# An adaptive-norm state-space block on one Trainium2 core: the small matmuls of a quad of head pairs in three atomic sections

## The chip, the core and the metric

The kernel runs on one core of a Trainium2 chip: TensorE (PE) with its weight loads (PEld), VectorE (DVE), ScalarE (ACT), GpSimd (POOL), and SyncE (SP), whose queue here issues the DMAs. TensorE writes its results to PSUM[...]. The metric is the device time of one execution in microseconds (us); the median of the runs counts.

## The reference

For 4 batches of 512 tokens with 256 channels: a normalisation with a shift and a scale from a small modulation network, a state-space mixer, a gated residual, a second normalisation, a feed-forward layer with a Hadamard transform, a second gated residual. The mixer is where the change lies:

```python
proj = u @ W_in.T
xBC, z, A_log = jnp.split(proj, [CONV_DIM, CONV_DIM + D_INNER], axis=-1)
...
x = x.reshape(b, l, NH, HEADDIM)
Bm = Bm.reshape(b, l, NH, D_STATE)
Cm = Cm.reshape(b, l, NH, D_STATE)
a = -jax.nn.softplus(A_log).transpose(0, 2, 1)
Lm = jnp.exp(segsum(a))
M = jnp.einsum('blhn,bshn,bhls->bhls', Cm, Bm, Lm)
y = jnp.einsum('bhls,bshp->blhp', M, x)
y = y + D[None, None, :, None] * x
```

There are 32 heads of 8 channels with a state of 64. Before this, xBC passes a causal convolution of four taps along the tokens.

## The kernel before

Everything is float32. The sum over earlier tokens is cut into 8 chunks of 64 tokens. Within a chunk the product of C and B, times the decays, is applied to x (**intra**). Across chunks, each chunk gives a state (**states**), the states are carried on by a scan (**turn_states**), and the products of C with the carried state are added (**inter**).

Work comes in *pairs* of heads, k = 0 to 63. Four pairs make a *quad*, m = 0 to 15; two quads make a *unit*, n = 0 to 7, which is half of the heads of one batch. For a pair:

- `project` (lines 447 to 455) computes B (half 0, PSUM tile pbc) and C (half 1, pcc), each by six full matmuls 512 wide (line 266), and `conv` (400 to 407) applies the convolution: two ACT operations from PSUM, two DVE operations, one POOL operation. The results are bc (3 buffers) and cc (8 buffers).
- `turn_b` (475 to 481) transposes B into bts (tag bt, 6 buffers).
- `prep_l` (440 to 445) makes the decays lts (tag l, 6 buffers): one matmul, one exponential on ACT.
- `attend` (457 to 473), once for two pairs, multiplies C and B chunk by chunk in two m banks (pG): 4 matmuls per chunk, 32 in all, each on a 64 by 64 piece of the array. A class `Chain` keeps them in order among themselves; other matmuls may come between. DVE then multiplies pG into lts (line 473).

For a quad: `states` (540 to 550) runs 16 matmuls on 128 by 32 pieces into one m bank (ps), and ACT copies it to st; `intra` (552 to 565) runs 32 on 128 by 32 pieces into the unit's bank py; `turn_states` (567 to 579) transposes st, scans it on DVE, and POOL writes it to sts; `inter` (581 to 591) runs 28 on 128 by 32 pieces into the unit's bank pi. A float32 matmul shows as two instructions in the trace, so a quad has 32 ps, 64 py and 56 pi, and an `attend` 64 pG.

PSUM: three banks for projections (tag p), three for everything of short life (tag m: pG, ps, the transposes bT, sT, xt and pt, the decays pl, the output products), one each for py and pi.

The order is made in two steps. The code is traced by an agenda: each piece has a due time in units of a pair (table `T`, line 414, and lines 784 to 841), and the pieces are traced in order of due time. Then a scheduler that models the engines' times orders each engine's instructions: among those whose inputs and buffers are there, the earlier traced goes first. So a later piece can slip into an earlier one. Only SP keeps its traced order. Where a tag has no free buffer, the writer waits until all readers of an old one are done.

Due times for quad m: states at 4m + 3.97, intra at 4m + 4.1, turn_states at 4m + 5.47, inter at 4m + 6.53. For pair k: attend (k odd) at k + 0.12, turn_b at k + 0.13, the projections at k - 1.11 and k - 1. After the mixer, the feed-forward part (from line 706) fills the last 135 us.

Of the kernel before, what the change touches and what calls it, by code (L numbers as in the profile page):

```python
# [16 lines left out]
AF = mybir.ActivationFunctionType  # L17
# [6 lines left out]
Q = 64  # L24
NC = S // Q
# [5 lines left out]
def mamba_ffn(tc, ctx, u, c_t, wmod, win_t, cw, cb, zb, dsk, wo_t, w13_t, w2_t,  # L31
              k_ident, k_reset, k_dl, k_dr, k_had, k_own, out):
    nc = tc.nc
    ve, ac, gp, pe = nc.vector, nc.scalar, nc.gpsimd, nc.tensor
# [14 lines left out]
    def at_time(t, fn, *args):  # L49
        heappush(agenda, (t, next(ids), fn, args))  # L50
# [9 lines left out]
    def work(shape, name, tag, bufs=2, dtype=F32):  # L60
        return wk.tile(shape, dtype, name=name, tag=tag, bufs=bufs)

    def mtile(shape, name):
        return ps_m.tile(shape, F32, name=name, tag="m")
# [97 lines left out]
    xpad = const.tile([128, 2, NC, 4, 32], F32, name="xpad")  # L162
    sts = [const.tile([128, NC - 1, 4, 32], F32, name=f"sts{pp}") for pp in range(2)]
    xwz = const.tile([128, 4, 16, 2, 8], F32, name="xwz")
# [100 lines left out]
        for n, (a, b, k) in enumerate(TERMS):  # L265
            last[pe] = pe.matmul(ps, w[:, a, k, c0 : c0 + 128], ht[k][:, b], start=(n == 0), stop=(n == 5))  # L266

    class Chain:

        def __init__(self):  # L270
            self.before = None

        def matmul(self, *args, **kw):
            with ExitStack() as order:
                if self.before is not None:
                    order.enter_context(tc.issue_after(self.before.ins))
                self.before = pe.matmul(*args, **kw)  # L277

    def normalize(b, which, x):
        mv = work([128, 4, 2], f"mv{which}{b}", "mv")  # L280
        rs = work([128, 4], f"rs{which}{b}", "rs")
        xn = work([128, 4, DM], f"xn{which}{b}", "xn", 1)
        for t in range(4):
            bs = work([128, 6], f"bs{which}{b}{t}", "bs")
            ve.bn_stats(bs, x[:, t])
            ve.bn_aggr(mv[:, t], bs)
        ve.tensor_scalar(rs, mv[:, :, 1], EPS, None, ALU.add)
        last[gp] = gp.tensor_tensor(rs, rs, neghalf, ALU.pow)
        if (b, which) == (0, 0):
            for t in range(4):  # L290
                ve.tensor_scalar(xn[:, t], x[:, t], mv[:, t, 0:1], rs[:, t : t + 1], ALU.subtract, ALU.mult)
            return xn
        nm = work([128, 4], f"nm{which}{b}", "nm")
        ve.scalar_tensor_tensor(nm, mv[:, :, 0], -1.0, rs, ALU.mult, ALU.mult)
        for t in range(4):
            ac.activation(xn[:, t], x[:, t], AF.Identity, bias=nm[:, t : t + 1], scale=rs[:, t : t + 1])  # L296
        return xn
# [102 lines left out]
    def conv(ps, tl, dst):  # L400
# [9 lines left out]
    NP = 64  # L410
# [2 lines left out]

    T = dict(
        attend=0.12, turn_b=0.13, prep_l=-1.31, proj_b=-1.11, proj_c=-1, load_d=-3.13,
        states=-0.03, intra=0.1, turn=1.47, inter=2.53,
        x_proj=1.32, x0=-1.5, x1=2.12, x2=3.46, x3=3.77, gate_z=5.89, fin0=3.54, fin1=3.96, fin2=4.99, fin3=6.63,
        pro0=-11.83, pro1=-7.06, pro2=-4.93, pro3=-4.48, pro4=-3.88, next_ht=-3.77, pro04=0.27,
        quads=1.55, xz1=32.3, wo=19.68, mod=18.99, w2=40.89, wf0=56.74, wf1=62.02, wf2=62.29,
        load_w2=63.01, w2tag=1, w2gp=0, first_h2=59.14, lag=4.89, next_h2=-2.27,  # L420
    )
# [5 lines left out]
    lts, bcs, ccs, bts, exs, des, xcs, xds, dcs, stt, pys, zts = ({} for _ in range(12))  # L427
# [29 lines left out]
    def attend(k):  # L457


        ks = (k - 1, k)  # L460
        pgs = [mtile([128, S], f"pG{n}") for n in ks]
        chain = Chain()
        for c in range(NC):


            for n, pg in list(zip(ks, pgs))[::-1]:
                for j in range(2):
                    i, o = 64 * j, 64 * (j ^ (n % 2))
                    r, l = slice(i, i + 64), slice(Q * c, Q * c + Q)
                    chain.matmul(pg[o : o + 64, l], bcs[n][r, l], ccs[n][r, l], start=True, stop=True,  # L470
                                 tile_position=(i, o))
        for n, pg in zip(ks, pgs):
            ve.tensor_tensor(lts[n], pg, lts[n], ALU.mult)  # L473

# [62 lines left out]
                                 wdec[b][:, 2 * hf + t, :, 16 * i : 16 * i + 16]  # L537
                                 .unsqueeze(3).to_broadcast([128, 2, 16, 8]), ALU.mult)

    def states(m):  # L540
        pp = m % 2
        pst = mtile([128, 4, 128], f"ps{m}")
        for t in range(4):
            for g in range(4):
                pe.matmul(pst[32 * g : 32 * g + 32, t], xwz[:, t, 4 * g + 2 * pp : 4 * g + 2 * pp + 2].rearrange("p h q x -> p (h q x)"),  # L545
                          bts[4 * m + g][:, t], start=True, stop=True, tile_position=(0, 32 * g))
        for g in range(4):
            bts.pop(4 * m + g)
        stt[m] = work([128, 4, 128], f"st{m}", "st", 1)
        ac.activation(stt[m], pst, AF.Copy)  # L550

    def intra(m):
        n, pp = divmod(m, 2)
        if pp == 0:
            pys[n] = (ps_1.tile([128, S], F32, name=f"py{n}", tag="y"),
                      ps_1.tile([128, S], F32, name=f"pi{n}", tag="yi"))
        py = pys[n][0]
        for c in range(NC):
            for g in range(4):
                l = slice(Q * c, Q * c + Q)  # L560
                pe.matmul(py[32 * g : 32 * g + 32, l], xpad[:, pp, c, g], lts[4 * m + g][:, l],  # L561
                          start=(pp == 0 and c == 0), stop=(pp == 1), skip_group_check=True,
                          tile_position=(0, 32 * g))
        for g in range(4):
            lts.pop(4 * m + g)

    def turn_states(m):
        n, pp = divmod(m, 2)
        st = stt.pop(m)
        pt = mtile([128, 4, 16, NC], f"sT{m}")  # L570
        for t in range(4):
            pe.transpose(pt[:, :, :, 2 * t : 2 * t + 2].rearrange("p g (h x) q -> p (g h) q x", h=2), st[:, t], ident)
        sn = work([128, 4, 16, NC], f"sn{m}", "xd", 2)
        ve.tensor_tensor_scan(sn.rearrange("p g x c -> p (g x c)"),
                              dcs[n][:, 8 * pp : 8 * pp + 8].rearrange("p h x c -> p (h x c)"),
                              pt.rearrange("p g x c -> p (g x c)"), 0.0, ALU.mult, ALU.add)
        o = 16 * pp
        gp.tensor_tensor(sts[pp][:, :, :, o : o + 16].rearrange("p c g x -> p g x c"), sn[:, :, :, : NC - 1],
                         own.unsqueeze(3).to_broadcast([128, 4, 16, NC - 1]), ALU.mult)

    def inter(m):
        n, pp = divmod(m, 2)
        pi = pys[n][1]
        for c in range(1, NC):
            for g in range(4):
                l = slice(Q * c, Q * c + Q)
                pe.matmul(pi[32 * g : 32 * g + 32, l], sts[pp][:, c - 1, g], ccs[4 * m + g][:, l],  # L587
                          start=(pp == 0 and c == 1), stop=(pp == 1), skip_group_check=True,
                          tile_position=(0, 32 * g))
        for g in range(4):  # L590
            ccs.pop(4 * m + g)

    def gate_z(n):
        i, b = units[n]
        pz = ptile(f"pz{n}")
        proj(pz, wxz[i], 128, ht[i, b])
        zt = work([128, S], f"zt{n}", "zt", 1)
        zz = work([128, S], f"zz{n}", "zz", 1)
        ac.activation(zt, pz, AF.Tanh, bias=hzb[:, i : i + 1], scale=0.5)
        ac.activation(zz, pz, AF.Identity, bias=zb_sb[:, i : i + 1])  # L600
        ve.scalar_tensor_tensor(zt, zt, 1.0, zz, ALU.add, ALU.mult)
        zts[n] = zt
# [179 lines left out]
        split_xz(1, fetch_xz(1))  # L782

    for m in range(16):
        at_time(4 * m + 4 + T["states"], states, m)
        at_time(4 * m + 4 + T["intra"], intra, m)
        at_time(4 * m + 4 + T["turn"], turn_states, m)
        at_time(4 * m + 4 + T["inter"], inter, m)
        if m:
            at_time(4 * m + T["load_d"], load_d, m)  # L790
    for k in range(NP):
        if k % 2:
            at_time(k + T["attend"], attend, k)
        at_time(k + T["turn_b"], turn_b, k)
        if k >= AHEAD:
            at_time(k + T["proj_b"], project, k, 0)
            at_time(k + T["proj_c"], project, k, 1)
        if k >= LOOK_P:
            at_time(k + T["prep_l"], prep_l, k)
# [106 lines left out]
```

## Time and profile before

| | us |
|---|---|
| median of 3 runs | 590.82 |
| lowest, highest | 587.2, 591.58 |
| the profiled execution | 587.27 |
| its span, first to last instruction | 585.5 |
| busy over the span: PE, PEld | 547.6, 431.7 |
| busy over the span: DVE, ACT, POOL | 400.5, 392.8, 325.6 |

A busy time is the sum over an engine's instructions; overlapping matmuls are counted once. Lines of groups and timelines name the source line (L277), the engine, the operation, the tile written and the tiles read, and the sizes; for matmuls "64*64" is the piece of the array in use. In the views of waits a line says which instruction stood still, which engine and tile released it, and the total, the number of times and, where there is a third number, the longest time.

### The profile page before, as it was taken

The page shows a single profiled execution, that of the slowest core. Times are in us where ns is not written, and L with a number is a line of the kernel's source. Part 1 is how long each engine was busy: PE and PEld are TensorE (multiplying, and loading weights), DVE is VectorE, ACT ScalarE, POOL GpSimd, SP SyncE. Part 2 cuts the span into 40 slices and gives each one's busy share as a digit, 9 for nine tenths or more (in the row PEclk, how much of TensorE's full clock was granted, in tenths as well). Part 3 has the DMA queues.
Part 4 walks back from the last instruction along what each step waited for, and adds up shares of the span by engine and source line. Part 5 has one row for each costly group of instructions (what it writes and reads, how often), then busy time and mean ns, then how long its engine had stood idle before and what let it go on. Part 6 is the DMA issues. An engine that isn't in the chain of part 4 may idle for free.

```text
span 585.5 us, 16297 instructions
## 1 busy us (share of the span) xinstructions
PE 547.6 (94%) x6868; PEld 431.7 (74%) x6868; DVE 400.5 (68%) x668; ACT 392.8 (67%) x670; POOL 325.6 (56%) x299
## 2 busy tenths in 40 slices
PE   6887999989899999999999899899989999999996
PEld 3555776668677766877777677677767898888886
DVE  4777877877787875889787879787855454333243
ACT  6898778877967887897794887769574243232321
POOL 4773356454734578466565657477666645333341
PEclk9898999999999999999999999999989999999999
DMA  6423111210325344013203142164158046104021
GB/s 195 137 53 151 33 37 74 47 34 1 110 50 84 115 123 142 3 59 103 80 4 113 75 119 97 60 172 147 38 158 284 2 131 209 40 1 152 1 82 36
DMA packets 41792, 51.99 MB, mean 89 GB/s; under 512 B 17942, under 2 KB 29940, under 8 KB 41720
## 3 DMA queue, kind: packets, MB, share of 16 engines
q1 hardware_dynamic: 40248, 50.58, 28.6%
q8 instruction: 54, 0.88, 0.6%
q10 hardware_dynamic: 1472, 0.38, 0.3%
q14 instruction: 18, 0.15, 0.1%
HBM read 33.51 MB, written 17.44 MB: 87 GB/s over the span
## 4 chain that ended last, share of the span: by engine, by line
PE 40%; DVE 5%; ACT 4%; issue 1%; POOL 1%; DMA 1%; POOLq 0%; DVEq 0%
PE f L266 15%; PE pdy L728 4%; PE pcc L266 4%; PE pdyi L728 4%; PE pbc L266 3%; PE po L625 2%; PE pG L277 1%; PE py L561 1%; PE bT L479 1%; ACT xn L296 1%; PE ps L545 1%; PE pi L587 1%; DVE cc L405 1%; PE pt L306 1%; ACT cv L404 1%
## 5 line engine op out<-in xcount | busy, mean ns | idle before, releaser
L407 POOL TENSOR_TENSOR bc<-bc,cv 128x509 f32<-128x509 f32 x64 | 69.6, 1088 | 58.7 <-DVE bc L406 41.4
L266 PE MATMUL f<-h,wf 128*128 128x512 f32 x384 | 97.3, 395 | 0.0
L407 POOL TENSOR_TENSOR cc<-cc,cv 128x509 f32<-128x509 f32 x64 | 69.7, 1089 | 49.2 <-DVE cc L406 33.4
L266 PEld LDWEIGHTS f<-h,wf 128*128 128x128 f32 x384 | 69.0, 189 | 12.3
L721 POOL TENSOR_TENSOR fl<-ft,fh 128x512 fp32r<-128x512 f32 x31 | 40.0, 1292 | 57.6 <-ACT fh L720 52.0
L405 DVE SCALAR_TENSOR_TENSOR cc<-pcc,cw_sb,cc 128x511 f32<-128x511 f32 x64 | 47.6, 743 | 31.0 <-ACT cv L404 30.9
L402 ACT ACTIVATE cc<-pcc,cb_sb,cw_sb 128x512 f32<-128x512 f32 x64 | 50.2, 785 | 20.6 <-PE pcc L266 15.1
L266 PE MATMUL pcc<-ht,wq 128*128 128x512 f32 x192 | 55.5, 421 | 5.8 <-DVE bc L406 5.8
L402 ACT ACTIVATE bc<-pbc,cb_sb,cw_sb 128x512 f32<-128x512 f32 x64 | 50.1, 783 | 15.3 <-PE pG L277 14.0
L720 ACT ACTIVATE fh<-ft 128x512 fp32r<-128x512 f32 x32 | 20.2, 631 | 57.7 <-DVE ft L717 28.7
L716 DVE SCALAR_TENSOR_TENSOR ft<-ft,f 128x512 f32<-128x512 f32 x32 | 21.9, 687 | 52.2 <-ACT ft L715 50.0
L405 DVE SCALAR_TENSOR_TENSOR bc<-pbc,cw_sb,bc 128x511 f32<-128x511 f32 x64 | 47.6, 744 | 12.8 <-ACT cv L404 12.6
L266 PE MATMUL pcc<-hr,wq 128*128 128x512 f32 x192 | 53.3, 410 | 2.9 <-DVE bc L406 2.3
L266 PE MATMUL pbc<-ht,wq 128*128 128x512 f32 x192 | 53.0, 408 | 2.6 <-POOL wq L199 2.6
L266 PE MATMUL pbc<-hr,wq 128*128 128x512 f32 x192 | 52.4, 406 | 1.4 <-DVE cc L406 1.0
L266 PEld LDWEIGHTS pcc<-ht,wq 128*128 128x128 f32 x192 | 35.8, 196 | 18.0 <-DVE bc L406 8.0
L406 DVE SCALAR_TENSOR_TENSOR bc<-pbc,cw_sb,bc 128x510 f32<-128x510 f32 x64 | 47.6, 743 | 1.2
L406 DVE SCALAR_TENSOR_TENSOR cc<-pcc,cw_sb,cc 128x510 f32<-128x510 f32 x64 | 47.6, 744 | 1.1
L473 DVE TENSOR_TENSOR l<-pG,l 128x512 f32<-128x512 f32 x64 | 41.2, 683 | 7.8 <-PE pG L277 7.5
L479 PE MATMUL bT<-ident,bc 128*128 128x128 f32 x256 | 41.2, 283 | 4.3 <-ACT bt L481 2.6
L404 ACT ACTIVATE cv<-pbc,cw_sb 128x512 f32<-128x512 f32 x64 | 44.4, 693 | 1.4 <-POOL bc L407 0.9
L481 ACT ACTIVATE bt<-bT 128x512 f32<-128x512 f32 x64 | 38.8, 607 | 9.4 <-PE bT L479 9.2
(154 smaller groups left out, 1237.0 us busy)
## 6 DMA issues: line engine op xcount, KB each, us to landing
wq<-win_t SPq DMA_DIRECT2D x16, 256.0 KB
htd<-ht SPq DMA_DIRECT2D x8, 512.0 KB
hr<-htd SPq DMA_DIRECT2D x8, 512.0 KB
h2d<-ht SPq DMA_DIRECT2D x8, 512.0 KB
h<-h2d SPq DMA_DIRECT2D x8, 512.0 KB
x<-u SPq DMA_DIRECT2D x7, 512.0 KB
ex<-pd SPq DMA_DIRECT2D x8, 256.0 KB
ygd<-yg SPq DMA_DIRECT2D x4, 512.0 KB
```

What stands on the lines that cost most here:

```text
L266: last[pe] = pe.matmul(ps, w[:, a, k, c0 : c0 + 128], ht[k][:, b], start=(n == 0), stop=(n == 5))
L402: ac.activation(dst, ps, AF.Identity, bias=cb_sb[:, tl : tl + 1], scale=w[:, 3:4])
L404: last[ac] = ac.activation(v, ps, AF.Copy, scale=w[:, 0:1])
L405: ve.scalar_tensor_tensor(dst[:, 1:], ps[:, : S - 1], w[:, 2:3], dst[:, 1:], ALU.mult, ALU.add)
L406: last["conv"] = ve.scalar_tensor_tensor(dst[:, 2:], ps[:, : S - 2], w[:, 1:2], dst[:, 2:], ALU.mult, ALU.add)
L407: last[gp] = gp.tensor_tensor(dst[:, 3:], dst[:, 3:], v[:, : S - 3], ALU.add)
L473: ve.tensor_tensor(lts[n], pg, lts[n], ALU.mult)
L479: pe.transpose(pt[:, t], bc[:, 128 * t : 128 * t + 128], ident)
L481: ac.activation(bts[k], pt, AF.Copy)
L716: ve.scalar_tensor_tensor(t, t, 1.0, p1, ALU.add, ALU.mult)
L721: (ve if (b, f) == (NB - 1, 7) else gp).tensor_tensor(lo, t, hi.bitcast(F32), ALU.subtract)
L728: last[pe] = pe.matmul(pds[t // 2][:, t % 2], hid[a][:, tok], w2h[f][:, w_], start=(f == 0 and t % 2 == 0 and m == 0), stop=(f == 7 and m ...
```

## The change

`states` and `intra` become one function, `states_intra`, whose matmuls are in one atomic section: to the scheduler it is a single unit that nothing can be put between, that starts when all its inputs are there, and that is done when all of it is. `attend` gets such a section around its matmuls in place of `Chain`. In every second `attend` of a quad, from the second quad on, the section begins with `inter` of the quad before; the last quad's `inter` has a section of its own. The due time of states goes, that of intra serves both; inter has a due time of its own only for the last quad. C's buffers are released behind the section (`drop_c`). The matmuls, their number and their data are the same.

```diff
-    class Chain:
...
-        states=-0.03, intra=0.1, turn=1.47, inter=2.53,
+        intra=0.1, turn=1.47, inter=2.53,
...
         pgs = [mtile([128, S], f"pG{n}") for n in ks]
-        chain = Chain()
-        for c in range(NC):
-            for n, pg in list(zip(ks, pgs))[::-1]:
-                for j in range(2):
...
-                    chain.matmul(pg[o : o + 64, l], bcs[n][r, l], ccs[n][r, l], start=True, stop=True,
-                                 tile_position=(i, o))
+        m = (k - 7) // 4 if k % 4 == 3 else -1
+
+        with tc.tile_critical():
+            if m >= 0:
+                inter(m)
+            for c in range(NC):
+                for n, pg in list(zip(ks, pgs))[::-1]:
+                    for j in range(2):
...
+                        pe.matmul(pg[o : o + 64, l], bcs[n][r, l], ccs[n][r, l], start=True, stop=True,
+                                  tile_position=(i, o))
+        if m >= 0:
+            drop_c(m)
...
-    def states(m):
...
-    def intra(m):
...
+    def states_intra(m):
+        n, pp = divmod(m, 2)
         pst = mtile([128, 4, 128], f"ps{m}")
...
+        with tc.tile_critical():
+            for t in range(4):
+                for g in range(4):
+                    w = xwz[:, t, 4 * g + 2 * pp : 4 * g + 2 * pp + 2].rearrange("p h q x -> p (h q x)")
+                    pe.matmul(pst[32 * g : 32 * g + 32, t], w, bts[4 * m + g][:, t], start=True, stop=True,
+                              tile_position=(0, 32 * g))
+            for c in range(NC):
+                for g in range(4):
+                    l = slice(Q * c, Q * c + Q)
+                    pe.matmul(py[32 * g : 32 * g + 32, l], xpad[:, pp, c, g], lts[4 * m + g][:, l],
+                              start=(pp == 0 and c == 0), stop=(pp == 1), skip_group_check=True,
+                              tile_position=(0, 32 * g))
         for g in range(4):
+            bts.pop(4 * m + g)
             lts.pop(4 * m + g)
+        stt[m] = work([128, 4, 128], f"st{m}", "st", 1)
+        ac.activation(stt[m], pst, AF.Copy)
...
+    def drop_c(m):
         for g in range(4):
             ccs.pop(4 * m + g)
+
+    def last_inter():
+        with tc.tile_critical():
+            inter(15)
+        drop_c(15)
...
-        at_time(4 * m + 4 + T["states"], states, m)
-        at_time(4 * m + 4 + T["intra"], intra, m)
+        at_time(4 * m + 4 + T["intra"], states_intra, m)
         at_time(4 * m + 4 + T["turn"], turn_states, m)
-        at_time(4 * m + 4 + T["inter"], inter, m)
...
+    at_time(NP + T["inter"], last_inter)
```

More of the change, by code (lines that the diff above doesn't have):

```diff
@@ L266, in proj @@
             last[pe] = pe.matmul(ps, w[:, a, k, c0 : c0 + 128], ht[k][:, b], start=(n == 0), stop=(n == 5))
-    class Chain:
[L270 to L277, printed above, removed]
     def normalize(b, which, x):
@@ L461, in attend @@
         pgs = [mtile([128, S], f"pG{n}") for n in ks]
-        chain = Chain()
-        for c in range(NC):
-            for n, pg in list(zip(ks, pgs))[::-1]:
-                for j in range(2):
-                    i, o = 64 * j, 64 * (j ^ (n % 2))
-                    r, l = slice(i, i + 64), slice(Q * c, Q * c + Q)
-                    chain.matmul(pg[o : o + 64, l], bcs[n][r, l], ccs[n][r, l], start=True, stop=True,
-                                 tile_position=(i, o))
+        m = (k - 7) // 4 if k % 4 == 3 else -1
[5 more added lines that the diff above has]
+                    for j in range(2):
+                        i, o = 64 * j, 64 * (j ^ (n % 2))
+                        r, l = slice(i, i + 64), slice(Q * c, Q * c + Q)
+                        pe.matmul(pg[o : o + 64, l], bcs[n][r, l], ccs[n][r, l], start=True, stop=True,
+                                  tile_position=(i, o))
+        if m >= 0:
+            drop_c(m)
         for n, pg in zip(ks, pgs):
@@ L538, in x_part3 @@
                                  .unsqueeze(3).to_broadcast([128, 2, 16, 8]), ALU.mult)
-    def states(m):
-        pp = m % 2
+    def states_intra(m):
+        n, pp = divmod(m, 2)
         pst = mtile([128, 4, 128], f"ps{m}")
[L543 to L550, printed above, removed]
-    def intra(m):
-        n, pp = divmod(m, 2)
         if pp == 0:
@@ L557, in intra @@
         py = pys[n][0]
[L558 to L563, printed above, removed]
+        with tc.tile_critical():
[10 more added lines that the diff above has]
+                              tile_position=(0, 32 * g))
         for g in range(4):
+            bts.pop(4 * m + g)
             lts.pop(4 * m + g)
+        stt[m] = work([128, 4, 128], f"st{m}", "st", 1)
+        ac.activation(stt[m], pst, AF.Copy)
     def turn_states(m):
```

## The prediction

> **What bounds the kernel now.** I first split the span by engine at the point where the feed-forward part takes over (busy time by stage; columns: stage, its length, then PE, PE's weight loads, DVE, ACT, POOL).
>
> ```profile
> 60.00:450.00 390.00, 370.14 (x5704) 284.78 (x5693) 306.78 (x501) 302.59 (x522) 235.56 (x216) 1.00 0.30 88
> 450.00:585.50 135.50, 130.53 (x818) 115.26 (x817) 53.14 (x88) 40.11 (x66) 56.24 (x46) 1.00 0.23 74
> ```
>
> The change works between about 39 and 452 us. There PE shows 370 of 390 us busy, DVE and ACT 79% and 78%. The later 135 us hold none of the edited work but the last inter, so I leave them alone. Matmul ends are modelled, so I read PE by the starts of its instructions, in the timeline of PE:
>
> ```profile
> 205.72 1.65 PE L266 MATMUL pcc<-ht,wq 128*128 128x512 f32 x6
> 207.31 1.16 PE L277 MATMUL pG<-cc,bc 64*64 64x64 f32 x64
> 208.40 0.66 PE L479 MATMUL bT<-ident,bc 128*128 128x128 f32 x4
> ...
> 64.21 0.33 PE L277 MATMUL pG<-cc,bc 64*64 64x64 f32 x4
> 64.47 1.66 PE L266 MATMUL pz<-ht,wxz 128*128 128x512 f32 x6
> 66.07 1.15 PE L277 MATMUL pG<-cc,bc 64*64 64x64 f32 x60
> ...
> 83.01 0.31 PE L545 MATMUL ps<-bt,xwz 128*32 128x128 f32 x3
> 83.03 0.30 PE L561 MATMUL py<-l,xpad 128*32 128x64 f32 x2
> 83.14 0.29 PE L545 MATMUL ps<-bt,xwz 128*32 128x128 f32 x3
> ```
>
> 64*64 and 128*32 are pieces of the array; 128*128 is all of it. Start to start, 512-wide matmuls follow each other every 0.231 us (median); the step from one into a 64*64 or 128*32 matmul is 0.318 to 0.327. Inside pG a step is 0.015 (0.943 us for 64). From the last pG to the transpose behind it 0.149. So a visit to the split array costs 0.09 going in and 0.134 coming out, 0.224 us. The weight loads say the same, as idle time that no other engine releases (first line, of the pG tile; it is 0.34 us each). And twice a visit is made for 4 matmuls alone, as at 64.21: 11 of the 32 pG groups start so.
>
> ```profile
>   issue: 10.6, 31
> ```
>
> Counting changes of shape in PE's order, the whole trace has 97 visits from the full array (57 to 128*32, 40 to 64*64; two of the 57 are the decays' pa alone, two more hold pi with pa behind it) and 3 direct steps from 128*32 to 64*64: some 22 us of PE time. Third, PE's waits in 60:450, and what ACT's line 402 waits for:
>
> ```profile
> PE pcc L266 <- DVE bc L406: 4.9, 12, 1.1
> PE pt L306 <- ACT bt L481: 3.4, 2, 1.7
> PE bT L479 <- ACT bt L481: 2.6, 5, 0.8
> PE pl L443 <- DVE sn L574: 2.2, 3, 0.8
> ...
>   PE pG L277: 14.0, 14
>   PE pi L587: 4.8, 7
> ```
>
> The first is a wait for one of three projection banks, the other three for one of three "m" banks. The last two lines are ACT waiting to write bc (3 buffers) until pG has read an old one, and to write cc (8 buffers) until pi has. So PE sets the pace, with bank and buffer releases close behind it.
>
> **What the Trainium skill says.** "TensorEngine Tiling (Array Packing)", Key Properties: changing the tiling mode, not merely the tile, drains TensorE. The 0.318 and 0.149 us steps agree. "TensorE: Matmul & The Clock Gate", Part 3, The mechanism: matmuls start and end in order, and a weight load is pulled ahead of running matmuls where its rows differ. The first agrees with every row here; so a matmul that waits holds all behind it. "PSUM — Partial Sum Buffer", Engine vs sequencer instructions: a standalone barrier belongs on a drain, which waits until the engine is fully idle. The trace before has no such barrier between its matmuls; this matters for the sections' ends.
>
> **The change, part by part.** Sections after: 16 states_intra, 32 attend (15 with inter in front), 1 last inter, 49 in all.
>
> *Visits removed.* 49 sections and the 4 pa groups make 53 visits. 97 - 53 = 44 fewer x 0.224 = -9.9 us. Direct steps from inter to pG become 15 instead of 3: 12 x 0.134 = +1.6. Together -8.3.
>
> *Order within states and intra.* Mixed, as at 83.01, 92 matmuls take 1.885 us; 32 ps alone take 0.809 (at 313.70), 32 py alone 0.435, so 92 in order take about 1.63. Seven quads x 0.25 = 1.8; those in two halves (2 x 0.895 against 0.81 + 0.88) give 0.1 each, 0.6. Together -2.4.
>
> These -10.7 us are PE time. With PE busy 95% of the stage I count 0.9 of it on the path: -9.6. What hides the rest is PE's own waits above.
>
> *The ends of a section.* As a unit it starts when its last input is there and reports when it is done. Not shown before. Lower bound nothing: the change of shape drains the array anyway. Upper: the last matmul runs to its end (0.219) and two PE semaphore instructions (0.051 each in the trace) and a weight load that can't be pulled ahead (0.135) are added, less the 0.149 already paid: 0.31 x 49 = 15. I take 0.08 each, +4, because the drain is mostly the one already paid.
>
> *Banks.* The 11 groups that begin with 4 pG hold two of three m banks for about 1.7 us while PE projects, and states begun on its first half hold one for some 4 us (59.74 to 63.96, 111.83 to 116.21). A section takes them only when it can run through. PE's waits on m banks in 60:450 are pt 3.4, bT 2.6 + 0.5, pl 2.2 + 1.0, hd 1.2, xt 0.5: 11.4. Bounds 0 and -11, taken -3. That states' result now waits for intra too, 0.9 us, costs nothing: the copy st feeds sT, which runs later (st at 218.71, sT at 225.31).
>
> *Later releases.* Inter moves from 4m + 6.53 to attend at 4m + 7.12. Now pi starts 0.9 to 6 us before the pG that it joins (75.80 and 78.31; 152.87 and 156.52), 3.0 on average over 15 quads. ACT can write cc of pair 4m + 8 only after pi: at 76.81 it starts as pi ends (76.79). In the joined section it starts at pG's end, some 3 us later, together with the bc that waits for pG. Until then a projection bank stays full. Behind it on ACT nothing need wait, as the order is laid out for it; on PE, pbc two pairs on wants the bank. Per quad: nothing, if transposes, pl or the next states_intra fill the place; 2 us, if PE stands as long as the conv is late. x 15: 0 to +30. I take a tenth, +3.5, as ACT and DVE have a fifth of their time free to catch up. A section's front also waits: while it stands for POOL's cc, the bT, pl and projections behind it stand too, and ACT's bt and l behind those; but pG waited for the same cc before. No DMA, and nothing on SP's or POOL's queue, is moved. The gating that reads pi has slack: pi(1) ends at 101.13, and the y bank that gating then frees is next written at 111.83.
>
> Sum: -9.6 + 4 - 3 + 3.5 = -5.1 us. The profiled run took 587.27 (span 585.5 and 1.8 around it), the low end of the runs; the median is 590.82. -5.1 gives 582.2 from one and 585.7 from the other; I say **584**.
>
> **Rivals.**
> 1. *Late buffers* (slower). The joined section is the place: cc and bc buffers come free together at its end, both convs queue on ACT (2 x 1.4 us), and PE runs out of projection banks. For: the 14.0 and 4.8 us waits, and the 4.9 us of PE behind them. Against: 15 to 20% of ACT and DVE free. It decides from 0.6 us of PE standing per quad (8.6 us saved elsewhere over 15); at 1.2 us it gives +9: 599.
> 2. *The ends eat the gain* (no change). At 0.2 us per section, 49 x 0.2 = 10 replaces the 4: about 590; at the bound of 0.31, 595. For: 49 places. Against: the drain is already in the 0.149.
> 3. *The banks were the real cost* (much faster). All of the 11 us of m-bank waits go, and PE time converts whole: -10.7 - 11 + 4 + 2 = -16: 573. For: the 11 early starts; against: PE fills those holds with projections.
> That the sections don't gather the work is excluded by what a section is; but the scheduler's whole order moves with them, for which I allow 4 us either way in each case.
>
> **Numbers.** Forecast 0.50 (own range 577 to 589), rival 1 0.20, rival 2 0.15, rival 3 0.15. The range 570 to 601 reaches to rivals 1 and 3. One per cent, 5.9 us, is what this measurement can tell from nothing. Faster: 0.35 of the forecast's half and all of rival 3, 0.50. Same: 0.15 + 0.07 + 0.02 = 0.24. Slower: 0.18 of rival 1 and 0.08 of rival 2, 0.26.
>
> **What would show it.** The steps into and out of pG, pi, ps and py number about 53; pG never comes as 4 and 60; ps and py don't mix. If the step out of a section is well above 0.149 us, rival 2. If ACT's line 402 waits for pG or pi far beyond 19 us in sum and PE's pbc or pcc wait on DVE beyond 7, rival 1. If PE's waits on ACT bt and DVE sn or l vanish, rival 3. The forecast is wrong if the count falls and PE's time between 60 and 450 doesn't.

## The result and the profile after

The changed kernel takes **756.55 us** (median of 5 runs, 752.44 to 762.73) against 590.82: ratio 1.2819, 95% interval 1.2746 to 1.2891. The forecast of 584 us (570 to 601) was wrong, in sign and by far in size. The profiled execution has a span of 754.2 us.

Busy time by stage, for the stretch with the sections and the one behind it (length; then PE, weight loads, DVE, ACT, POOL; granted clock; DMA):

```profile
60.00:621.00 561.00, 416.15 (x5861) 321.95 (x5865) 312.69 (x520) 313.20 (x537) 238.25 (x219) 0.90 0.20 62
621.00:754.00 133.00, 128.12 (x765) 113.02 (x754) 52.20 (x85) 38.97 (x64) 54.77 (x44) 0.99 0.22 72
```

The feed-forward part is as long as before. The mixer has grown by two fifths, though no engine has more to do: DVE, ACT and POOL are about as busy in sum as before, with longer pauses between. PE has the same matmuls; it shows 416 us where it showed 370, in part because its granted clock is 0.90 on average where it was 1.00.

Who stood still, longest first, in the waits of all engines ("PEld" is PE's weight loads, "PEq" PE's sequencer; L453 and L540 are the functions that hold the sections of attend and of states_intra):

```profile
DVE l L466 <- PEq L453: 142.0, 31, 13.3
...
ACT cc L391 <- PEq L453: 78.2, 13, 13.6
...
ACT st L556 <- PEq L540: 62.1, 16, 11.2
...
PEld pi L578 <- issue: 43.8, 16, 9.3
PEld ps L544 <- issue: 40.2, 16, 7.8
...
PEld pG L461 <- issue: 33.4, 23, 7.7
ACT bc L391 <- PEq L453: 31.1, 13, 8.0
```

In the waits before, two of these places:

```profile
DVE l L473 <- PE pG L277: 7.5, 8, 2.3
ACT st L550 <- PE ps L545: 13.6, 8, 5.0
```

Before, the "issue" line for pG was 10.6 us in 31 pieces of a third of a microsecond. Now pi, ps and pG, the first tiles of the three sections, wait 117 us together and up to 9 us at a time, and "issue" names no releaser. In the waits of PE alone, transfers that these sections don't read stand as releasers:

```profile
PE pG L461 <- DMA htd<-ht: 7.5, 1, 7.5
PE ps L544 <- DMA ygd<-yg: 7.4, 1, 7.4
```

What PE does there stands in the view of the line to which the section's own instructions are put:

```profile
L897 PEldq EVENT_SEMAPHORE  x296: 51/51/8572, 41.7 to 754.2; - x148
L897 PEldq COMPARE_BRANCH  x49: 163/168/301, 49.1 to 619.5; - x49
```

Duration in ns, shortest/median/longest. Six semaphore instructions for each of the 49 sections (294 of the 296), and a branch. The kernel before has no branch there, and semaphore instructions only ahead of the matmul that needs them. The compiled program's list of PE instructions names what they wait for (not a profile; the first section with inter and attend, cut; the twelve waits of the six semaphore instructions and the one of the branch are written as the branch's):

```
NoOp [waits DVE, PE_sequencer, Activation, Pool]
Matmult bT_1067<-ident,bc_925 128x128 [waits Pool]
UnconditionalBranch [waits DMAHW2, DMAHW1, DMAHW3, DMAHW0, DMAHW4, PE_sequencer, DMAHW5, DVE, DMAHW6, PE, DMAHW7, Activation, Pool]
Matmult pi_739<-cc_300,sts_139 32x64
...
```

The NoOp holds inputs of the section itself. The branch into the section waits for *everything*: the eight counters DMAHW0 to DMAHW7, which the transfers take in turn, those of DVE, ACT and POOL, PE's own matmuls and its sequencer. In the program of the changed kernel, all 49 branches wait for the last count handed out ahead of them, on all thirteen. One place of the 49, in the timeline of PE:

```profile
371.65 0.27 PE L472 MATMUL bT<-ident,bc 128*128 128x128 f32 x1
380.88 1.72 PE L578 MATMUL pi<-cc,sts 128*32 128x64 f32 x56 [8.95 <-issue]
382.53 1.76 PE L461 MATMUL pG<-cc,bc 64*64 64x64 f32 x64
```

in that of SP, which issues the DMAs:

```profile
370.61 2.62 SPq L317 DMA_DIRECT2D hr<-htd  x2
```

and in busy time by stage:

```profile
370.00:374.00 4.00, 1.93 (x9) 1.26 (x7) 2.31 (x4) 1.00 (x3) 2.69 (x4) 1.00 0.91 212
374.00:378.00 4.00, 0.00 (x0) 0.00 (x0) 0.00 (x0) 0.00 (x0) 0.99 (x2) 0.88 1.00 350
378.00:382.00 4.00, 1.12 (x44) 1.13 (x48) 0.00 (x0) 0.00 (x0) 0.00 (x0) 0.50 0.19 61
```

SP has just issued two loads of 512 KB (hr, the activations of a later unit). The section reads cc, sts and bc, never hr. It still waits for them: the second load landed at 380.01, and the semaphore instruction at which PE's sequencer had stood for 8.57 us, the longest of the view above, ended at 380.04. Meanwhile DVE, ACT and POOL, which live on PE's output, stop too. By then the clock has dropped to 0.50, and the pG that took 1.16 us before takes 1.76.

Where the 165 us lie, from the starts of PE's instructions between the first pG and the last pi (an account of mine from the two traces; after it takes in the 7.7 us in front of the first pG; us in sum, number, mean):

| step from one matmul to the next | before, 414 us | after, 579 us |
|---|---|---|
| into pG, ps, py or pi | 27.9 (94, 0.297) | 115.7 (49, 2.361) |
| out of them | 17.2 (95, 0.181) | 21.1 (48, 0.440) |
| inside them | 75.1 | 93.7 |
| behind a 512-wide matmul | 218.2 (844) | 267.0 (892) |
| others | 75.8 | 81.8 |

The way in makes 88 of the 165. Taken apart by the counter at which PE's sequencer stood (an account from the trace, too; nearly every wait of over 0.1 us ended within 0.1 us of the last update of its counter), the 115.7 us are some 44 at the DMA counters, 21 at those of the engines, PE's own among them, 17 ahead of the six semaphore instructions, for the section's own inputs and banks, and 34 in which nothing is waited for. The 512-wide row has 49 more: some 11 for 48 more matmuls that fall in the window, some 10 for steps at the halved clock, and the rest waits, for the most part for a projection bank, that is for convolutions. That these are late because of a section is likely, as their engines stop at the sections, but not traced. Inside, 19 us are the halved clock.

### The profile page after: what moved, and what is told of

It reads as the page before. It is cut to its first block, busy times and chain, and to the rows that moved or that the text cites. A ratio compares the mean times of both kernels' runs of the same rounds, so it can differ in the third digit from the quotient of the medians.

```text
span 754.2 us, 16964 instructions
## 1 busy us (share of the span) xinstructions
PE 586.4 (78%) x6867; PEld 462.3 (61%) x6868; DVE 397.6 (53%) x668; ACT 394.5 (52%) x670; POOL 324.6 (43%) x299
## 5 line engine op out<-in xcount | busy, mean ns | idle before, releaser
L266 PE MATMUL pbc<-hr,wq 128*128 128x512 f32 x192 | 56.9, 435 | 12.7 <-DVE cc L395 10.1
L461 PE MATMUL pG<-cc,bc 64*64 64x64 f32 x2048 | 44.7, 248 | 25.2 <-DMA htd<-ht 7.5
L266 PE MATMUL pbc<-ht,wq 128*128 128x512 f32 x192 | 54.8, 421 | 11.5 <-DVE cc L395 4.6
L461 PEld LDWEIGHTS pG<-cc,bc 64*64 64x64 f32 x2048 | 39.9, 159 | 34.2 <-issue 33.4
L472 PE MATMUL bT<-ident,bc 128*128 128x128 f32 x256 | 47.8, 300 | 11.4 <-PEq L453 2.7
L266 PEld LDWEIGHTS pbc<-hr,wq 128*128 128x128 f32 x192 | 37.3, 204 | 25.7 <-ACT cv L393 10.8
L578 PE MATMUL pi<-cc,sts 128*32 128x64 f32 x896 | 20.4, 257 | 39.1 <-issue 11.4
L266 PEld LDWEIGHTS pbc<-ht,wq 128*128 128x128 f32 x192 | 36.4, 199 | 22.9 <-ACT cv L393 4.5
L544 PE MATMUL ps<-bt,xwz 128*32 128x128 f32 x512 | 23.0, 336 | 34.1 <-DMA ygd<-yg 7.4
```

Source lines behind the costliest of these rows:

```text
L461: pe.matmul(pg[o : o + 64, l], bcs[n][r, l], ccs[n][r, l], start=True, stop=True, tile_position=(i, o))
L472: pe.transpose(pt[:, t], bc[:, 128 * t : 128 * t + 128], ident)
L544: pe.matmul(pst[32 * g : 32 * g + 32, t], w, bts[4 * m + g][:, t], start=True, stop=True, tile_position=(0, 32 * g))
```

## The experiments

The theories: **A**, the border of a section costs, because PE waits at it for all that was given to every engine and DMA queue before; **B**, the joining and the late release of C's buffers cost (the prediction's first rival); **C**, a border has a fixed price alone.

**Borders without joining** (e1_borders). The kernel before, in which one matmul of each group has a section:

```diff
+                    if (c, n, j) == (0, k, 0):
+                        with tc.tile_critical():
+                            pe.matmul(pg[o : o + 64, l], bcs[n][r, l], ccs[n][r, l], start=True, stop=True,
+                                      tile_position=(i, o))
+                        continue
                     chain.matmul(pg[o : o + 64, l], ...
...
+              with tc.tile_critical() if (t, g) == (0, 0) else ExitStack():
                 pe.matmul(pst[32 * g : 32 * g + 32, t], ...
```

> The kernel before, with a section around one single matmul at each of the 49 places (the first pG of every attend, the first ps of every states, the first pi of the last quad); nothing is joined or moved. Theory A (a section's borders: at its entry PE waits for all that every engine and every DMA queue had been given before it, plus a fixed price of some 0.7 to 0.9 us): most of the 166 us come back without any joining, 690 to 780 us. Theory B (late buffers, the joining itself): the borders cost little, at most 49 x 0.3 = 15 us, so below 610. Theory C (only the fixed price of a border, 49 x 0.86 = 42 us): about 630.

698.73 us, ratio 1.1816 (1.1744 to 1.1889): 110 us come back from borders that gather nothing, 2.2 us each. So joining isn't the main cause (B), and a fixed price as small as the 42 us expected for 49 borders isn't either (C); what the fixed price is comes below.

**Joining without borders** (e2_joined, e2b_chained). The changed kernel with its groups, due times and `drop_c`; in the second the groups keep their inner order:

```diff
-        with tc.tile_critical():
+        with ExitStack():
...
-                        pe.matmul(pg[o : o + 64, l], ...
+                        chain.matmul(pg[o : o + 64, l], ...
```

> The changed kernel with its joining, due times and later release of C's buffers, but no section around the matmuls. Theory A: the loss is gone, 575 to 605 us. Theory B: the loss stays, above 720. Theory C: 754 less 42, about 712.

> As e2_joined, with the order inside each of the three groups held by Chain (each matmul issued behind the one before, others may come between). Theory A: 570 to 600 us, and a little below e2_joined if mixing of ps and py and changes of the array's shape cost what the prediction counted (2 to 6 us). Theory B: above 720. Theory C: about 712.

597.74 us, ratio 1.0119 (1.007 to 1.0168), and 588.93 us, 0.999 (0.9966 to 1.0014). Without the sections the loss is gone; the order inside the groups, which the second run holds, is worth 9 us. The joining costs ACT's bc a little, as the waits of ACT in e2b_chained show; it was 14.0 in 14 before:

```profile
ACT bc L402 <- PE pG L277: 17.0, 17, 1.9
```

**Part of the sections** (e3_attend, 32 around attend alone, and e7_states_intra, 16 around states and intra alone; the rest as before).

> The kernel before with sections around the 32 attends alone; states, intra and inter stay as they were. Theory A: 32 of 49 sections, so about 32/49 of 166 = 108 us more: 699, between 660 and 730. Theory B (the joining of inter and the late C buffers are not there): below 605. Theory C: 32 x 0.86 = 28 more, about 618.

> The kernel before with the changed kernel's section for states and intra alone (16 sections); attend and inter stay. Theory A, a cost per section: 16 of 49, so 16/49 x 166 = 54 us more, 643, between 620 and 665. The 32 attends alone cost 89; the two and the joining together should come near the 166. Theory C (fixed price): 16 x 0.86 = 14, about 603.

677.67 us, ratio 1.1451 (1.1383 to 1.1519), and 667.43 us, 1.131 (1.1265 to 1.1356). Together 89 + 78 = 167, against 166 for all 49. Theory A holds, but not as a flat cost: 2.8 us for a section of attend, 4.9 for one of states_intra. The latter comes ahead of st, the state's copy on ACT, which waited 13.6 us for ps before; the waits of e7_states_intra:

```profile
ACT st L563 <- PEq L547: 92.4, 16, 14.3
```

Which part of the difference is the late inputs of the longer section, and which the moment at which it comes, these two runs don't separate.

**The fixed price** (e4_back2back). 32 sections behind the last output, when nothing is under way:

```diff
+    z = ps_1.tile([128, S], F32, name="z_end", tag="y")
+    for _ in range(32):
+        with tc.tile_critical():
+            pe.matmul(z, idle[:, :128], idle, start=True, stop=True)
```

> The kernel before with 32 sections back to back behind its last output, each around one full 512-wide bf16 matmul on zeros; nothing else is left to wait for but the last stores. It measures the fixed price of a border. Theory A: from one section's matmul to the next some 0.9 to 1.3 us (matmul 0.2 to 0.4 included), 30 to 42 us in all. If a section costs 3.4 us of itself (166/49), about 110 us in all.

645.44 us in one run, 57 more than before. From one matmul to the next it is 1.85 us on average, more than the 0.9 to 1.3 expected and far less than 3.4. In the timeline of PE:

```profile
602.75 0.61 PE L845 MATMUL z_end<-idle 128*128 128x512 bf16 x1 [1.25 <-PEq L844]
604.86 0.61 PE L845 MATMUL z_end<-idle 128*128 128x512 bf16 x1 [1.50 <-issue]
```

The clock is 0.50 there. At that clock 512-wide matmuls follow each other every 0.427 in the changed kernel (at 622), so by estimate some 0.43 is the matmul's own step and 1.4 the border: drain, six semaphore instructions of 0.106 from start to start, branch, weights. In the changed kernel cheap borders come to some 0.5 going in and 0.18 coming out beyond the old steps. By these two, 49 borders cost an estimated 33 to 69 us even if nothing is waited for, so theory C holds for a part; what is left of the 110 of e1_borders is waiting.

**A transfer that has nothing to do with the section** (e5_transfer0 and 1, e6_two_copies0 and 1). In the feed-forward part SP copies 2 MB within DRAM, once or twice; in the second of each pair three matmuls a little behind have a section:

```diff
+        if s_ == 18:
+            junk = dram.tile([128, 8, 2, DM], F32, name="junk")
+            nc.sync.dma_start(junk, w2d)
...
+            with tc.tile_critical() if (b, f, t) == (2, 3, 0) else ExitStack():
                 for m, (a, w_) in enumerate(PASSES):
```

> Control: the kernel before with one 2 MB copy within DRAM, which nobody reads, issued in the feed-forward part. All theories: PE does not wait for it beyond what later loads on the same queue are late, within 15 us of before.

> The same copy, and one section around three matmuls of the feed-forward part that is reached soon after the copy was issued; the matmuls have nothing to do with it. Theory A (the entry waits for every DMA queue): PE stands in front of the section until the copy has landed, one gap of 8 us or more that ends as it lands. Theories B and C: no gap above 1.5 us there.

> Control: two 2 MB copies within DRAM, one behind the other, in the feed-forward part, no section. All theories: no gap of PE at the place of the section of the next run; later loads may be late, within 25 us of before.

> The same two copies and one section around three matmuls soon behind them. One copy gave PE a gap of 3.05 us, ending about when the DMA engines fell idle. Theory A: the gap grows by the time of the second copy, some 8 to 12 us, to 11 to 15, and again ends as the DMA engines fall idle. If the gap is a price of the border it stays at 3.

One run each. With one copy PE's gap is 3.05 us, not the 8 expected: its sequencer waited for 5.65 us, but the matmuls already queued covered the first part. With two it is 9.62, somewhat under the 11 to 15. The controls have no gap at that place (592.65 and 589.87 us; with the section 596.68 and 598.86). The timeline of PE in e6_two_copies1:

```profile
548.95 0.79 PE L729 MATMUL pdy<-w2h,fh 128*128 128x256 f32 x2 [9.62 <-issue]
```

and its busy time by stage, with PE first, then the clock, the DMA share and GB/s last:

```profile
540.00:542.00 2.00, 0.00 (x0) 0.00 (x0) 0.05 (x1) 0.00 (x0) 0.00 (x0) 1.00 1.32 459
542.00:544.00 2.00, 0.00 (x0) 0.00 (x0) 0.00 (x0) 0.00 (x0) 0.00 (x0) 0.80 0.19 66
...
546.00:548.00 2.00, 0.00 (x0) 0.00 (x0) 0.00 (x0) 0.00 (x0) 0.00 (x0) 0.50 0.71 90
548.00:550.00 2.00, 1.05 (x4) 0.93 (x4) 0.00 (x0) 0.00 (x0) 0.00 (x0) 0.50 0.00 0
```

The control, e6_two_copies0, at a like place with its copies under way:

```profile
544.00:546.00 2.00, 2.00 (x12) 1.70 (x11) 0.25 (x1) 0.82 (x2) 1.29 (x1) 1.00 1.44 492
```

With the section all engines idle, the DMA engines are at work until about 548, and PE starts once they are done. The copies, which nobody reads, landed at 540.79 and 546.38, and two loads issued behind them, which the section doesn't read, at 547.57 and 548.09. PE's sequencer had stood at a DMA counter since 535.90, and went on at 548.12. So the end of the wait is the last load's, and the copies lengthen it by holding up what comes behind them. It is the same with one copy: the copy landed at 544.57, the last load at 546.42, and the sequencer went on at 546.46.

**What can be had without sections** (e8_chain_si, e9_late_first). States and intra as one group in the order of Chain, with attend and inter as before; then the same group turned round, py first and from the operand that comes last:

```diff
-        with tc.tile_critical():
+        chain = Chain()
...
-            for c in range(NC):
-                for g in range(4):
+            for c in reversed(range(NC)):
+                for g in (3, 2, 1, 0):
```

(The first change is that of e8_chain_si against states_intra; the second is what e9_late_first adds.)

> The kernel before with states and intra as one group at intra's due time, ordered by Chain (all ps, then all py) and without a section; attend and inter stay as before. In PE's order the visits to the split array fall from 97 to 81. Theory A with the prediction's own prices: 16 x 0.224 + 2.4 for the mixing = -6 us of PE time, 580 to 586 us. If PE's steps between shapes are not on the path: no change, 587 to 591. If states waiting for intra costs something: above 592. Against e2b_chained, which joins inter with attend as well, it shows what that joining costs.

> e8_chain_si with the order inside the group turned: py first, from the pair and chunk whose inputs come last, then ps from its last quarter; so the group's inputs are there when it begins, and the m bank of ps is taken at its end. The visits to the split array fall from 81 to 74. If the gain of e8_chain_si comes from fewer visits and shorter held banks, a little more of it: 578 to 585 us. If that gain was only another order by chance: 585 to 592.

585.75 us, ratio 0.9921 (0.9891 to 0.9951): the only version here that beats the kernel before, by 0.8% where 6 us (1%) were priced. And 602.58 us, 1.0218 (1.017 to 1.0265), against what was expected of it: fewer visits still, and slower by 17 us. The waits of PE in e9_late_first show a part of it; the line is new:

```profile
PE py L277 <- DVE xpad L532: 6.5, 4, 2.8
```

A group that begins with its last input waits at its front with PE idle. These 6.5 us are not the whole: ACT's st, too, waited 30.5 us for ps, which now comes last, against 12.7 in e8_chain_si, and what the rest consists of stays open. So the order within a group can cost more than gathering earns, without any border.

## Why the prediction was wrong

*What bounds the kernel.* Right: PE sets the pace, and the mixer alone changed.

*Visits.* The count was right: 53 entries from the full array and 15 direct steps, as counted. Their price is at least not contradicted: the direct step from pi to pG is 0.149, and e8_chain_si gives 4.7 us where 6 were priced for 16 fewer visits and sorted ps and py. By the order of starts its trace has 77 visits, 20 fewer than 97, which at the same price makes nearly 7. A gain of this size exists; in the changed kernel it was buried.

*Order within states and intra.* 96 matmuls in order take 1.755 us at full clock in the changed kernel; scaled from the prediction's parts, 1.69.

*The ends of a section: the step that failed.* The prediction put 0.08 us on a section, 4 us in sum, with an upper bound of 0.31 and 15. Measured: the way in is 2.06 us longer on average (2.361 less 0.297) and the way out 0.26 (0.440 less 0.181), and 49 borders, gathering nothing, cost 110 us. The working took the drain for the main cost and added up a drain, two semaphore instructions and a weight load. What it didn't ask is what the entry *waits for*. It wrote that a section starts when its last input is there; here it started only when all work handed out before it was done, DMAs included: 44 us at DMA counters and 21 at those of the engines, of the 115.7 on the way in. The bound was therefore no bound: none of the terms could hold a wait for another engine. And "No DMA, and nothing on SP's or POOL's queue, is moved" was beside the point, because what those queues had been given became a gate. The fixed part was too small as well: even cheap borders cost 0.5 going in and 0.18 coming out, above the bound of 0.31.

*Banks.* Not tested by itself. The two holds of ps's bank were read from the start of py at 59.74 and 111.83; ps itself starts at 60.21 and 112.30, which makes 3.7 and 3.9 us. In e9_late_first, which takes ps's bank only at the group's end, no gain is to be seen.

*Late releases.* The size fits, as far as it can be told: joining inter with attend costs the difference between e2b_chained (0.999) and e8_chain_si (0.992), 0.7%, some 4 us with an uncertainty of about 2, taken as 3.5. What the joining saves in visits is in that difference too.

*The rivals.* The first, late buffers, named the side but not the cause. The second named the place and stopped at 595, for the same reason that the bound was too low. The third, a larger gain, did not come.

*What went unasked.* That PE idles long enough to lose its clock: 19 us inside the small groups and some 10 behind 512-wide matmuls. "TensorE: Matmul & The Clock Gate", Part 1, of the Trainium skill says that the clock is halved after at least one idle window of about 3.4 us. Here it reads 0.88 in a stretch of 4 us that PE idles through and 0.50 in the next, and it stays low for 3.41, 6.83 or 10.24 us, which agrees with such a window. But less idling was enough: in the 7 us in front of 19 of the 26 such stretches of the changed kernel before its end, no single halt of PE had reached 3.4 us; the longest before the one at 203.0 was 1.42.

## What to carry to other kernels

Before work is put into an atomic section, ask what its entry waits for, not only what its matmuls need: if the list names DMA counters and engines whose work the section doesn't read, each section is a barrier for all of them, and its price depends on what happens to be under way. Order alone, each instruction issued behind the one before, gives a part of the grouping at no border: 77 visits in e8_chain_si, against 97 before and 53 with the sections. And a bound on an unseen cost is only one if every kind of cost is in it, a wait for others first of all.

## What the runs showed of the hardware that wasn't expected

- Back to back, with nothing else under way, a border costs some 1.4 us on PE (step of 1.85 less a matmul's 0.43 at half clock); its drain reads 0.33 us in the changed kernel (median) and each semaphore instruction takes 0.106 from start to start.
- A gap of 9.6 us in PE leaves the clock at 0.50 for about 4 us of matmuls after it: 548 to 552 in e6_two_copies1, and 0.64 in the two after that.
- In the changed kernel the clock stands at 0.50 for 140 us in sum, in 27 stretches; before, for 13 us in 4.
- The sequencer's wait and PE's gap differ by what is already queued: 5.65 us of waiting left a gap of 3.05 with one copy.
- Nearly every long wait of PE's sequencer at a border ended within 0.1 us of its counter's last update: hr landed at 380.01, and the wait ended at 380.04.
